# Moving the mixer's squares to another buffer, and bias, sines, filter banks and a normalization to other steps of the attention loop

## The chip, the core and the metric

The kernel runs on one core of one Trainium2 chip. The metric is the device time of one execution in microseconds. The kernel before takes 1604.8 us (median of three runs, 1603.25 to 1608.38). Everything is float32.

The core has engines that run side by side, each in its own order: TensorE (PE in the profile, with its weight loads as PEld), VectorE (DVE), ScalarE (ACT), GpSimd (POOL), and SyncE (SP), which here only issues DMAs. Engines wait for each other through semaphores.

## The reference, cut to what matters

Two layers on x of 8 sequences (b) of 1024 tokens with 128 channels.

```python
# layer 0: attention over the tokens of each sequence
x = x + conv_attn(group_norm(x))        # q, k l2-normalized over tokens; softmax(10 q k); w_out; + b_out
# layer 1, on tokens t
t = t + mamba(layer_norm(t)) + reversed(mamba'(reversed(layer_norm(t))))   # state-space mixer
t = t + spectral(layer_norm(t))         # 16 long filters as FFTs, banks M_phi mixed by 4 weights
```

Of the mixer, per sequence and direction: project to z, x, B, C and dt; a convolution of four taps and silu; a scan in chunks of 64 tokens with decays `exp(segsum(dt*A))`; add `D*x`; multiply by `silu(z)`; normalize by the mean of the squares; project out.

## The kernel before, in words

The program is one stream of instructions per engine. In the attention and the mixer the order is written out by hand: a `manual_schedule` keeps PE, DVE, ACT and POOL in the order in which the Python code emits them. Python generators (`qkv`, `mixer_and_bank`, `transforms`, `transform_taps`, `weighted`) hold side work that is advanced with `next(...)` at chosen steps, so the place of a `next` decides what an instruction stands behind on its engine.

**Attention.** `units` has 128 steps n: 8 sequences, two halves of 512 queries, 8 blocks of 128 keys. A step computes scores (`scores`, L618 on PE into PSUM `pt`, exponential L623 on ACT into `pr`), adds weighted values for the step before (`weigh`, L639), and at every second step sums pairs of `pr` on DVE (`two`, L648) for the denominators (L659). Beside this, by n modulo 16:

- `qkv(b)` prepares a later sequence: transposes (L536), copy (L538), statistics (L543), group norm's rsqrt on POOL (`gn`, L128 and L130) at step 3, scaling of `xnt` (L561, DVE) at 5, q at 6, the squares of q (L580, ACT) at 7, k at 10, the squares of k at 11 and then POOL's lengths (`inv`, L583 and L585), scaling of k (L600, DVE) at 13. The bias `bout` is added to X on POOL (L539), directly after the copy at step 14.
- `mixer_and_bank` (`mixing`): prepares mixer weights and mixes the filter banks M_u and M_phi of the spectral part with weights from a softmax (`select_bank`, a chain of tiny DVE instructions, L214 to L240). The mixing itself is POOL work: `mixed` (L251 and L253) and `both` (L272). It has 32 pieces; seven are advanced per 16 steps.
- `transforms` (`making`) computes angle tables: integers by POOL, casts (L306), range reduction on DVE, sines on ACT (L300). `inv` and `fwd` get their sines before the loop, the four `lags` tables at n = 73.
- At n = 99 and 115 statistics for the mixer's first two sequences, at 103 and 119 the normalization itself (`normalized`, L454): eight activations on ACT in a row.

**Mixer.** 16 units (b, d), two directions for each sequence. A unit's order on PE around the change: transposes of x (`sx`), of B with the product of B and C (`sb`), for d = 0 with a sequence to follow also the transposes of its tokens (`px`); the decays between tokens of a chunk (`pl`, L932); for d = 0 the dt projection of the next sequence (`pd`, L488); decays from a chunk's start (`pe`, L950), chunk states (`pst`, L970), and later the outputs (`sy`, L1039). `between` turns `pl` into `lm` with an exponential on ACT (L939). `pl`, `pd` and `pe` take turns in two PSUM buffers (`ps_w`), so the first matmul after `pl` needs the first `lm` exponential to have read its buffer. ACT loads a table of functions before that exponential. `gate` writes the squares `u.sq` (L1063, ACT) from y; `square_sums` sums them on PE (`misc`, L1081) at the unit's end. All these tiles are from pools in which a tag names one buffer: `sq` has the tag `lm`, so squares and decays share a buffer.

Of the kernel before, what the change touches and what calls it, by code (L numbers as in the profile page):

```python
# [8 lines left out]
F32 = mybir.dt.float32  # L9
AF = mybir.ActivationFunctionType  # L10
ALU = mybir.AluOpType
# [3 lines left out]
P = 128  # L15
B = 8
T = 1024
NT = T // P
C = 128
# [25 lines left out]
def fast_kernel(ctx: ExitStack, tc: tile.TileContext, a: dict, out: bass.AP, bad: bass.AP):  # L45
# [252 lines left out]
    def sines(dst):  # L298
        dst = dst.rearrange("p k i m -> p (k i m)")
        nc.scalar.activation(dst, dst, AF.Sin, scale=-2048.0 * PI_1024)  # L300
# [8 lines left out]
    def transforms(pool, tables):  # L309

        odd = counted(pool, [2, NF], [[512, 2], [2, NF]], 1, 0, "odd")
        place = counted(pool, [4], [[1, 4]], 0, 4, "place")
        odd_row = counted(pool, [1], [[1, 1]], 1, 2, "odd_row")
        places = counted(pool, [4, P], [[1, 4], [4, P]], 0, 0, "places")
        lag = counted(pool, [2, 2], [[-256, 2], [1, 2]], 510, -2, "lag")
        for t in (place, odd_row, lag):
            nc.vector.tensor_scalar(t, t, 1.0 / 2048.0, None, ALU.mult)
        yield
        yield from angles(pool, inv, [(inv, places, odd_row[:, 0:1])], "inv")
        yield  # L320
        yield from angles(
            pool, fwd, [(fwd[:, k : k + 1], odd[:, 0:1, :], place[:, k : k + 1]) for k in range(4)], "fwd"
        )
        yield
        for h in range(2):
            for r in range(2):
                t = pool.tile([P, 2, 2, NF], F32, name=f"lags{h}_{r}")
                for _ in angles(pool, t, [(t, odd, lag[:, h, r : r + 1])], f"lags{h}_{r}"):
                    pass
                tables.append(t)  # L330
                yield
        for t in tables:
            sines(t)

    def transform_taps(pool, ps, tables):
# [113 lines left out]
    def normalized(b, pool, mv, rstd):  # L449
        shift = pool.tile([P, NT], F32, tag="ln_s", name=f"b_shift{b}")  # L450
        nc.vector.scalar_tensor_tensor(shift, mv[:, :, 0], -1.0, rstd, ALU.mult, ALU.mult)
        xn = pool.tile([P, NT, C], F32, tag="ln_x", name=f"b_x{b}")
        for j in range(NT):
            nc.scalar.activation(  # L454
                xn[:, j, :], X[b][:, j, :], AF.Identity, bias=shift[:, j : j + 1], scale=rstd[:, j : j + 1]
            )
        return xn

    n2 = 2 * NH
    pad = KC - 1  # L460
# [57 lines left out]
    with ExitStack() as s:  # L518
# [12 lines left out]
        def qkv(b):  # L531

            xin = X[b]
            pt = ps_t.tile([P, T], F32, tag="t", name=f"xt{b}")
            for j in range(NT):
                nc.tensor.transpose(pt[:, j * P : (j + 1) * P], xin[:, j, :], ident)  # L536
            xt = p1.tile([P, T], F32, tag="xnt", name=f"xnt{b}")
            nc.vector.tensor_copy(xt, pt)  # L538
            nc.gpsimd.tensor_tensor(xin, xin, bout.unsqueeze(1).to_broadcast([P, NT, C]), ALU.add)  # L539
            yield  # L540
            st = p2.tile([P, 2, 6], F32, tag="st", name=f"st{b}")
            for i in range(2):
                nc.vector.bn_stats(st[:, i, :], xt[:, i * 512 : (i + 1) * 512])  # L543
            mv = p2.tile([P, 2], F32, tag="mv", name=f"mv{b}")
            nc.vector.bn_aggr(mv, st.rearrange("p i s -> p (i s)"))
            yield
            pm = ps_t.tile([P, 1], F32, tag="t", name=f"pm{b}")
            nc.tensor.matmul(pm, lhsT=group, rhs=mv[:, 0:1], start=True, stop=True)
            mean = p2.tile([P, 1], F32, tag="mean", name=f"mean{b}")
            nc.vector.tensor_copy(mean, pm)  # L550
            dm = p2.tile([P, 1], F32, tag="dm", name=f"dm{b}")
            nc.vector.tensor_tensor(dm, mv[:, 0:1], mean, ALU.subtract)
            nc.vector.scalar_tensor_tensor(dm, dm, dm, mv[:, 1:2], ALU.mult, ALU.add)
            yield
            pv = ps_t.tile([P, 1], F32, tag="t", name=f"pv{b}")
            nc.tensor.matmul(pv, lhsT=group, rhs=dm, start=True, stop=True)
            var = p2.tile([P, 1], F32, tag="var", name=f"var{b}")
            nc.vector.tensor_copy(var, pv)
            rstd = rsqrt(p2, var, 1, 1.0, 1e-5, "gn")
            yield  # L560
            nc.vector.tensor_scalar(xt, xt, mean, rstd, ALU.subtract, ALU.mult)  # L561
            yield

            ss = p2.tile([P, 2], F32, tag="ss", name=f"ss{b}")
            for i, (name, dst) in enumerate((("q", qs), ("k", ks))):
                pq = ps_t.tile([P, T], F32, tag="t", name=f"p{name}{b}")
                for n in range(2):
                    nc.tensor.matmul(
                        pq[:, n * 512 : (n + 1) * 512],
                        lhsT=wqkv[:, i * C : (i + 1) * C],  # L570
                        rhs=xt[:, n * 512 : (n + 1) * 512],
                        start=True,
                        stop=True,
                    )
                to = keepq.tile([P, T], F32, tag=name, name=f"{name}{b}")
                nc.vector.tensor_copy(to, pq)
                dst.append(to)
                yield
                junk = p1.tile([P, T], F32, tag="junk", name=f"junk{name}{b}")
                nc.scalar.activation(junk, to, AF.Square, accum_out=ss[:, i : i + 1])  # L580
                if i == 0:
                    yield
            nc.gpsimd.tensor_scalar(ss, ss, 1e-24, None, ALU.max)  # L583
            lengths = p2.tile([P, 2], F32, tag="inv", name=f"inv{b}")
            nc.gpsimd.tensor_tensor(lengths, ss, mhalf.to_broadcast([P, 2]), ALU.pow)  # L585
            yield
            pvl = ps_t.tile([P, NT, P], F32, tag="t", name=f"pvl{b}")
            for j in range(NT):
                nc.tensor.matmul(
                    pvl[:, j, :],  # L590
                    lhsT=xt[:, j * P : (j + 1) * P],
                    rhs=wqkv[:, 2 * C : 3 * C],
                    start=True,
                    stop=True,
                )
            v = keepq.tile([P, NT, P], F32, tag="v", name=f"v{b}")
            nc.scalar.copy(v.rearrange("p j d -> p (j d)"), pvl.rearrange("p j d -> p (j d)"))
            vs.append(v)
            yield
            nc.vector.tensor_scalar(to, to, lengths[:, 0:1], lengths[:, 1:2], ALU.mult, ALU.mult)  # L600
# [90 lines left out]
        for at in range(10):  # L691
            next(coming)
            if at in (1, 2, 3, 4, 5, 7):
                next(making)
        for t in (inv, fwd):
            sines(t)
        next(coming, None)
        coming = qkv(1)
        next(coming)
# [1 line left out]
        for n in range(len(units) + 2):  # L701
# [16 lines left out]
                coming = qkv(n // 16 + 2)  # L718
            if n % 16 in (14, 15, 1, 3, 5, 6, 7, 10, 11, 12, 13):
                next(coming, None)  # L720
            if n % 16 in (0, 2, 4, 6, 8, 10, 14):
                next(mixing, None)
            if n >= 16 * (B - 1):
                next(going, None)
# [3 lines left out]
            if n in (99, 115):  # L728
                norm = normalize(bridge, n // 112)
            elif n in (103, 119):  # L730
                xns[n // 112] = normalized(n // 112, bridge, *norm)
            elif n == 113:
                turn_tokens(0, seqs[0], ps_t.tile([P, T], F32, tag="t", name="px0"))
            elif n == 117:
                sizes = steps(0, seqs[0], ps_t.tile([P, T], F32, tag="t", name="pd0"))
                next(sizes)
            elif n in (121, 123):
                next(sizes, None)
# [10 lines left out]
    with ExitStack() as s:  # L749
# [297 lines left out]
        def gate(u, n):  # L1047

            if n == 0:
                u.y = p1.tile([P, 2, T], F32, tag="y", name=f"y{u.tag}")  # L1050
                u.sq = p1.tile([P, 2, T], F32, tag="lm", name=f"sq{u.tag}")
            by_chunk = "p (j c l) -> p c j l"
            for c in range(2):
                nc.vector.scalar_tensor_tensor(
                    u.y[:, n, :].rearrange(by_chunk, j=NT, c=2)[:, c],
                    u.xs[:, n, :].rearrange(by_chunk, j=NT, c=2)[:, c],
                    dcol[u.d][:, n : n + 1],
                    u.py[c][:, n],
                    ALU.mult,
                    ALU.add,  # L1060
                )
            nc.vector.tensor_tensor(u.y[:, n, :], u.y[:, n, :], u.zs[:, n, :], ALU.mult)
            nc.scalar.activation(u.sq[:, n, :], u.y[:, n, :], AF.Square)  # L1063
# [69 lines left out]
        for at, u in enumerate(units):  # L1133
# [14 lines left out]
                going = steps(fresh, seqs[fresh], wide_psum(ps_w, f"pd{fresh}"))  # L1148
                next(going)
            if u.d == 1 and u.b + 2 < B:  # L1150
                xns[u.b + 2] = normalized(u.b + 2, bridge, *norms.pop(u.b + 2))
            from_start(u, 0)
            chunk_states(u)
            pass_states(u)
# [1122 lines left out]
```

## Time and profile before

| stretch (us from the start) | what | PE busy | DVE busy | ACT busy | POOL busy | granted clock |
|---|---|---|---|---|---|---|
| 0 to 32.7 | start, up to the first exponential | 13.18 | 22.60 | 9.06 | 15.92 | 0.93 |
| 32.7 to 472.5 | attention | 422.51 | 340.53 | 285.92 | 217.33 | 0.98 |
| 472.5 to 1153.7 | mixer | 634.43 | 518.18 | 374.62 | 109.00 | 0.97 |
| 1153.7 to 1606 | spectral part | 392.61 | 275.08 | 197.04 | 98.55 | 0.94 |

The rows come from the view of busy times by stretch; the span of the profiled execution is 1605.8 us. Read it from PE: in attention and mixer it is busy over nine tenths of the time, so what matters is the few microseconds at which PE stands still or runs at a lower clock, and who kept it. A granted clock of 1.00 is full speed.

### The profile page before, as it was taken

To read this page: it belongs to the slowest core of one execution; us is meant where nothing else is said; L and a number is where in the kernel's file an instruction comes from. 1 tells how busy PE (TensorE), PEld (TensorE's weight loads), DVE (VectorE), ACT (ScalarE), POOL (GpSimd) and SP (SyncE) were. 2 spreads that over 40 slices of the span, in tenths; PEclk is the share of its full clock that TensorE was granted. 3 is DMA by queue.
4 is the path that set the end of the run, shared out by engine and by line. 5 is a ranking of instruction groups with operands and counts; after the bars stand their busy time and mean duration, and the time that the engine had idled before them with its cause. 6 is when DMAs were issued, how large, how long until landed. Compare 5 with 4: busy or idle time off the path is not lost. (4 is left out here: it accounts for less than half of the span.)

```text
span 1605.8 us, 45749 instructions
## 1 busy us (share of the span) xinstructions
PE 1462.7 (91%) x20118; PEld 886.4 (55%) x20118; DVE 1156.4 (72%) x2314; ACT 866.6 (54%) x1229; POOL 440.8 (27%) x488
## 2 busy tenths in 40 slices
PE   5999999999997999999999999999477899999977
PEld 2323332332334565566565565555367899989862
DVE  6688988777665778787878778778453477777754
ACT  3756665766565456565565656555153265555530
POOL 3299899111110102121212121111064411111100
PEclk8999999999999899999999999999778999999988
DMA  6111121000000010101010010101157623223248
GB/s 164 34 31 50 53 67 40 1 1 1 1 1 13 2 27 14 27 14 28 14 25 16 14 27 14 27 14 27 42 174 208 194 53 82 73 63 86 70 117 309
DMA packets 131960, 89.05 MB, mean 55 GB/s; under 512 B 41480, under 2 KB 114824, under 8 KB 131752
## 3 DMA queue, kind: packets, MB, share of 16 engines
q1 hardware_dynamic: 129640, 81.84, 18.7%
q8 instruction: 160, 2.62, 0.7%
q10 hardware_dynamic: 2112, 4.19, 0.7%
q14 instruction: 48, 0.39, 0.1%
HBM read 44.60 MB, written 33.55 MB: 49 GB/s over the span
## 5 line engine op out<-in xcount | busy, mean ns | idle before, releaser
L623 ACT ACTIVATE pr<-pt 128x1024 f32<-128x1024 f32 x256 | 248.2, 1021 | 131.6 <-PE pt L618 124.5
L648 DVE TENSOR_TENSOR two<-pr,pr 128x1024 f32<-128x1024 f32 x128 | 163.4, 1317 | 14.9 <-ACT pr L623 13.6
L1349 DVE COPY gs<-pg 128x512 f32<-128x512 f32 x256 | 159.7, 686 | 20.0 <-PE pg L1338 13.0
L1351 ACT COPY gs<-pg 128x512 f32<-128x512 f32 x256 | 134.1, 599 | 71.6 <-PE pg L1338 53.1
L618 PE MATMUL pt<-q,k 32*128 32x512 f32 x1024 | 159.9, 656 | 11.0 <-ACT pr L623 6.6
L1338 PE MATMUL pg<-taps,mst 32*128 32x128 f32 x4096 | 150.7, 284 | 9.1 <-ACT gs L1351 4.9
L1338 PEld LDWEIGHTS pg<-taps,mst 32*128 32x128 f32 x4096 | 136.6, 190 | 23.4 <-issue 17.6
L639 PE MATMUL po<-pr,v 128*32 128x512 f32 x1024 | 144.2, 610 | 0.0
L824 DVE SCALAR_TENSOR_TENSOR xs<-xp,cw,xs 128x1024 f32<-128x1024 f32 x96 | 123.1, 1283 | 7.5 <-ACT xs L816 5.2
L1372 PE MATMUL py<-gs,u 128*32 128x128 f32 (+1 forms) x4096 | 127.9, 277 | 0.2 <-DVE gs L1349 0.2
L1372 PEld LDWEIGHTS py<-gs,u 128*32 128x32 f32 (+1 forms) x4096 | 112.1, 140 | 7.5 <-DVE gs L1349 0.4
L844 PE MATMUL pb<-bxt,wbc 128*128 128x512 f32 x256 | 114.2, 598 | 0.3 <-ACT zs L835 0.3
L1099 POOL TENSOR_TENSOR rms<-rms_v,mhalf 128x8 f32<-128x8 f32 x16 | 39.2, 2453 | 269.1 <-DVE rms_v L1097 269.1
L778 POOL TENSOR_TENSOR dau<-upto,da 128x2048 f32<-128x2048 f32 x16 | 57.9, 3620 | 158.9 <-DVE state L984 158.9
L618 PEld LDWEIGHTS pt<-q,k 32*128 32x128 f32 x1024 | 47.3, 187 | 89.9 <-issue 34.4
L1361 POOL TENSOR_SCALAR u<-u 128x512 f32<-128x512 f32 x16 | 24.0, 1498 | 233.7 <-PE pg L1338 119.9
L987 DVE SCALAR_TENSOR_TENSOR state<-state,dec,pst 128x64 f32<-128x64 f32 x448 | 87.3, 275 | 1.1
L659 PE MATMUL pd<-two,ones 128*32 128x512 f32 x512 | 78.8, 619 | 4.4 <-DVE two L648 4.0
L844 PEld LDWEIGHTS pb<-bxt,wbc 128*128 128x128 f32 x256 | 47.1, 189 | 56.0 <-issue 53.8
L639 PEld LDWEIGHTS po<-pr,v 128*32 128x32 f32 x1024 | 28.8, 110 | 89.1 <-issue 85.1
L950 PE MATMUL pe<-dau,ones 64*64 64x512 f32 x256 | 69.7, 668 | 8.8 <-ACT lm L939 6.6
L1039 PEld LDWEIGHTS sy<-lm,xdt 64*64 64x64 f32 x2048 | 59.9, 139 | 29.8 <-DVE ec L1013 15.2
(279 smaller groups left out, 2863.9 us busy)
## 6 DMA issues: line engine op xcount, KB each, us to landing
ud<-sp SPq DMA_DIRECT2D x8, 1024.0 KB
u<-ud SPq DMA_DIRECT2D x32, 256.0 KB
yd<-sums SPq DMA_DIRECT2D x32, 256.0 KB
moved<-state SPq DMA_DIRECT2D x48, 128.0 KB
yt<-yd SPq DMA_DIRECT2D x6, 1024.0 KB
X<-in_x SPq DMA_DIRECT2D x8, 512.0 KB
part_p<-in_L_ffn_M_phi_plus SPq DMA_DIRECT2D x32, 128.0 KB
part_m<-in_L_ffn_M_phi_minus SPq DMA_DIRECT2D x32, 128.0 KB
```

The lines of the kernel that those rows point to most:

```text
L618: nc.tensor.matmul(pt[:, i, :], lhsT=k[rows, j * P : (j + 1) * P], rhs=q[rows, cols], start=True, stop=True)
L623: nc.scalar.activation(pr[:, 2 * g : 2 * g + 2, :].rearrange("p i t -> p (i t)"), pt.rearrange("p i t -> p (i t)"), AF.Exp, scale=SCALE,)
L639: nc.tensor.matmul(po[rows, :], lhsT=vs[b][:, j, rows], rhs=pr[:, h, :], start=(j == 0), stop=(j == NT - 1))
L648: nc.vector.tensor_tensor(two, sums["pr"][:, 2 * g : 2 * g + 2, :], pr[:, 2 * g : 2 * g + 2, :], ALU.add)
L659: nc.tensor.matmul(sums["d"][(2 * g + i) * DH : (2 * g + i + 1) * DH, :], lhsT=ones[:, :DH], rhs=two[:, i, :], start=(j == 1), stop=(j == ...
L824: nc.vector.scalar_tensor_tensor(acc, xp[:, at : at + T], cw[u.d][:, n, i : i + 1], acc, ALU.mult, ALU.add)
L844: nc.tensor.matmul(u.pb[:, i * 512 : (i + 1) * 512], lhsT=wbc[u.d][:, k, :], rhs=xt[:, at : at + 512], start=(k == 0), stop=(k == KC - 1),)
L987: nc.vector.scalar_tensor_tensor(u.state[:, k, h, :], u.state[:, k - 1, h, :], u.dec[:, c, j, h : h + 1], u.pst[c][:, j, h, :], ALU.mult, ...
L1338: nc.tensor.matmul(pts[g][:, e, :], lhsT=mst[rows, n * 4 + e, :], rhs=taps[rows, cols].rearrange("p f q m i -> p (f q m i)"), start=True, ...
L1349: nc.vector.tensor_copy(to, frm)
L1351: nc.scalar.copy(to, frm)
L1372: nc.tensor.matmul(py[t * 32 : t * 32 + 32 - 16 * m, q // 2, :], lhsT=u[:, i, m:, :, :, q * FC + f].rearrange("p k b i -> p (k b i)"), rhs ...
```

## The change

The change has two parts. The squares of the mixer take the buffer of the decayed x (`xdd`), not that of the decays (`lm`). In the attention loop the bias addition goes from the copy at step 14 to after the squares of q at step 7; the sines of `inv` are emitted before the first squares of q and those of `fwd` together with the `lags` tables at n = 73; one cast and three scalings of the tables go behind the first sequence's copy and statistics; the mixing of the banks is advanced five times per 16 steps, at 4, 6, 8, 12 and 14 (so it ends at n = 102 instead of n = 72, and the DVE chain of `select_bank` goes from n = 14 to n = 22); and the mixer's normalization is split into halves, at n = 103 and 105, and at 119 and 122. No arithmetic is added or removed. The aim is that instructions that stand behind others on their engine, without needing them, no longer do.

```diff
@@ transforms
         places = counted(pool, [4, P], [[1, 4], [4, P]], 0, 0, "places")
+        yield
         lag = counted(pool, [2, 2], [[-256, 2], [1, 2]], 510, -2, "lag")
         for t in (place, odd_row, lag):
             nc.vector.tensor_scalar(t, t, 1.0 / 2048.0, None, ALU.mult)
-        yield
...
-        for t in tables:
+        for t in (fwd, *tables):
             sines(t)
@@ normalized
         for j in range(NT):
+            if j == NT // 2:
+                yield
             nc.scalar.activation(
@@ qkv
             nc.vector.tensor_copy(xt, pt)
-            nc.gpsimd.tensor_tensor(xin, xin, bout.unsqueeze(1).to_broadcast([P, NT, C]), ALU.add)
...
                 nc.scalar.activation(junk, to, AF.Square, accum_out=ss[:, i : i + 1])
                 if i == 0:
+                    nc.gpsimd.tensor_tensor(xin, xin, bout.unsqueeze(1).to_broadcast([P, NT, C]), ALU.add)
                     yield
@@ before the loop
-        for t in (inv, fwd):
-            sines(t)
+            if at == 4:
+                sines(inv)
@@ the loop
-            if n % 16 in (0, 2, 4, 6, 8, 10, 14):
+            if n % 16 in (4, 6, 8, 12, 14):
                 next(mixing, None)
...
-                xns[n // 112] = normalized(n // 112, bridge, *norm)
+                norming = normalized(n // 112, bridge, *norm)
+                next(norming)
+            elif n in (105, 122):
+                next(norming, None)
@@ gate
-                u.sq = p1.tile([P, 2, T], F32, tag="lm", name=f"sq{u.tag}")
+                u.sq = p1.tile([P, 2, T], F32, tag="xdd", name=f"sq{u.tag}")
```

More of the change, by code (lines that the diff above doesn't have):

```diff
@@ L451, in normalized @@
         nc.vector.scalar_tensor_tensor(shift, mv[:, :, 0], -1.0, rstd, ALU.mult, ALU.mult)
-        xn = pool.tile([P, NT, C], F32, tag="ln_x", name=f"b_x{b}")
+        xn = xns[b] = pool.tile([P, NT, C], F32, tag="ln_x", name=f"b_x{b}")
         for j in range(NT):
+            if j == NT // 2:
+                yield
             nc.scalar.activation(
@@ L456, in normalized @@
             )
-        return xn
     n2 = 2 * NH
@@ L1150, in fast_kernel @@
             if u.d == 1 and u.b + 2 < B:
-                xns[u.b + 2] = normalized(u.b + 2, bridge, *norms.pop(u.b + 2))
+                for _ in normalized(u.b + 2, bridge, *norms.pop(u.b + 2)):
+                    pass
             from_start(u, 0)
```

## The prediction

> **What bounds the kernel now.** I read the page first: PE is busy 91% of the span. The busy times by stretch then show that attention and mixer are PE's, and that POOL's load differs between sequences. Two sequences of the attention loop side by side, b = 3 and b = 5 (columns: stretch, its length, busy time of PE, PEld, DVE, ACT, POOL, granted clock, DMA):
>
> ```profile
> 194.70:251.00 56.30, 52.33 (x377) 17.50 (x380) 46.01 (x53) 34.12 (x37) 53.45 (x51) 1.00 0.20 57
> 306.20:356.20 50.00, 50.00 (x376) 16.63 (x379) 39.31 (x49) 34.01 (x37) 6.60 (x5) 1.00 0.00 1
> ```
>
> The same PE and ACT work takes 50.0 us where POOL is empty and 56.3 where it is full. Measured from exponential to exponential, the eight sequences (b = 0 to 7) take 51.7, 56.2, 54.1, 56.3, 55.2, 50.0, 55.0 and about 60 us; 50.0 is the floor. The timeline says who held PE:
>
> ```profile
> 160.86 0.94 DVE L561 TENSOR_SCALAR xnt<-xnt,mean,gn 128x1024 f32<-128x1024 f32 x1 [4.26 <-POOL gn L130]
> ...
> 161.95 1.95 PE L568 MATMUL pq<-xnt,wqkv 128*128 128x512 f32 x4 [2.27 <-DVE xnt L561]
> ...
> 381.44 3.18 ACT L454 ACTIVATE b_x<-X,b_shift,ln_r 128x128 f32<-128x128 f32 x8
> ```
>
> DVE sat 4.26 us for POOL's rsqrt, which stood behind mixing, and PE 2.27 us for DVE. Later ACT spends 3.18 us on the normalization at a stretch.
>
> ```profile
> 7.55 2.34 POOL L539 TENSOR_TENSOR X<-X,bout 128x1024 f32<-128x1024 f32 x1
> 7.59 2.32 DVE L306 CAST lag<-lag_i 128x4 f32<-128x4 int32 x1 [0.23 <-POOL lag_i L304]
> ...
> 27.54 2.35 POOL L539 TENSOR_TENSOR X<-X,bout 128x1024 f32<-128x1024 f32 x1
> 27.61 2.83 DVE L600 TENSOR_SCALAR k<-k,inv 128x1024 f32<-128x1024 f32 x1 [0.91 <-POOL inv L585]
> ```
>
> A cast of four columns lasts 2.32 us and the scaling of k 2.83 (its fastest is 0.71): both started just after a bias addition on POOL and ended with or just after it.
>
> In the mixer I asked for the decays' line and for one unit on ACT and PE:
>
> ```profile
> L939 ACT ACT_TABLE_LOAD  x16: 1283/1283/1283, 501.0 to 1122.5; - x16
> L939 ACTq EVENT_SEMAPHORE  x15: 17/17/17, 553.1 to 1122.4; - x15
> ```
>
> ```profile
> 715.53 0.58 ACT L910 COPY bk<-sb 128x512 f32<-128x512 f32 x1 [4.03 <-PE sb L902]
> 717.48 1.28 ACT L939 ACT_TABLE_LOAD   x1 [1.36 <-PE pl L932]
> 718.77 1.94 ACT L939 ACTIVATE lm<-pl 128x1024 f32<-128x1024 f32 x2
> ```
>
> ```profile
> 715.41 3.70 PE L932 MATMUL pl<-dau,row_lt 128*128 128x512 f32 x8
> 719.85 0.65 PE L950 MATMUL pe<-dau,ones 64*64 64x512 f32 x2 [0.73 <-ACT lm L939]
> ```
>
> The table load, which needs no data, waits 1.36 us for `pl`; the exponential comes after it, and PE idles 0.73 us for the buffer. This repeats in 15 of 16 units, those with an event semaphore at L939.
>
> ```profile
> 758.82:761.99 3.17, 2.12 (x18) 1.87 (x17) 0.25 (x2) 1.76 (x2) 0.00 (x0) 1.00 0.55 165
> 761.99:767.20 5.21, 5.21 (x73) 2.92 (x75) 0.59 (x3) 1.28 (x2) 0.00 (x0) 0.67 0.01 3
> 719.85:723.36 3.51, 3.51 (x72) 2.41 (x74) 0.27 (x2) 3.51 (x9) 0.00 (x0) 1.00 0.00 0
> ```
>
> In a d = 0 unit the idle gap is followed by `pd`, sixteen matmul records of eight columns; then `pe` and `pst` take 5.21 us at a mean clock of 0.67, against 3.51 at 1.00 in the d = 1 unit.
>
> [...]
>
> **The change part by part.**
>
> 1. *Squares in `xdd`'s buffer.* In the built order before, `lm`'s exponential has two waits, ACT's own earlier `sq` (same buffer) and PE's `pl`, and the one for `pl` is placed ahead of the table load. In the changed order `lm` has the wait for `pl` alone, directly at the exponential, and the table load has none. It can start when `bk` is copied, 716.11, and end by 717.39, before `pl`'s first half at 717.48. The exponential starts 717.48 instead of 718.77, its first half (1.02) ends at 718.50. `pl`'s last matmul starts at 718.52 and the next can follow about 0.43 later (their spacing), 718.95 instead of 719.85: 0.90 us. In d = 0 units the copy before is `bxt`, ended 755.88; load until 757.18, `pl` ready 757.35, so the same 0.90. Sum 15 x 0.90 = 13.5; the idle time alone is 15 x 0.73 = 11. The new sharing makes the next `xdd` wait for `misc`'s matmuls, but its own input `xdt` needs the transposes `sx` behind them on PE, so nothing is added; behind `xdd` on DVE stand `gm` and the residual, which then wait for nothing new. What follows on DVE (28 state steps of 0.2 to 0.3 us) starts from `pst`, thus moves with PE. I take 12.
>
> 2. *The clock in d = 0 units.* The nearly empty stretch goes from 3.17 to 2.27 us. [...] Six such units lose 5.21 - 3.51 = 1.7 us each, 10 in all. I take 7, range 0 to 10.
>
> 3. *Start.* Without cast and scalings ahead, the copy of the first `xnt` starts near 7.4 instead of 10.03; with 0.4 given back behind the statistics, group norm is 2.0 to 2.3 earlier. But the bias addition now stands right behind `gn` on POOL and meets L561: 0.81 becomes about 2.8, and 2.0 is lost[...]. L600 at 27.61 then meets an idle POOL, 0.8 instead of 2.83, and the first scores start 2.0 earlier. The exponential's table must be loaded by then: `inv`'s sine (1.06) lies in ACT's 21.1 us of idle time, `fwd`'s is gone from here, one table load less. I take -2.0 (0 to -4).
>
> 4. *Bias and mixing.* With pieces at 4, 6, 8, 12, 14 none is queued ahead of `gn` at 3 or the lengths at 11, and POOL gets 5/7 of the load. The 21.8 us above the floor in b = 1 to 4 hold 3.8 for the lags' sines, about 5 for the `select_bank` chain around n = 14 to 17, and about 13 for waits on POOL's queue and held `two`s. I expect 9 of the 13 back. b = 5 and most of b = 6 now have POOL work: +0.7 each, +1.4. The chain at n = 22 still delays av behind it but no longer stands behind a bias addition (L214 took 1.28): -2.
>
> 5. *Sines.* `fwd` at n = 73 stands between exponentials: 1.04 on ACT, +1.0.
>
> 6. *Normalization in halves.* The lump held PE 2.02 us at 385.57 and 2.60 at 448.42, and the clock was at half from there. A half is 1.6 us, of which the step's spare ACT time (2.9 less 2.0) takes about 0.9. I take -2.5 and -3.0.
>
> Sum: -12 - 7 - 2 - 9 + 1.4 - 2 + 1 - 5.5 = -35.1. 1604.8 - 35 = 1570. The spectral part isn't touched.
>
> **The rivals.**
> - *Clock not healed, half of the POOL gain*: -11 for the mixer's gaps, -11 for attention: 1583. For it: [...]most bank work still meets DVE.
> - *Everything at its upper value*: -13.5 - 10 - 22 = 1559. For it: every PE gap named is one with PE as head of the chain.
> - *Mixer bound elsewhere*: PE's gap reappears at a wait for DVE or ACT (`pp` waits for `ec` 0.34 us per unit already), so only attention gains, 12: 1593. Against: DVE idles 3.49 us before the state copy.
> - *Slower*: bias additions meet `two` or L561 in every sequence (8 x 2.0 = +16), b = 5 and 6 rise by 3 each, `fwd` +1, and the mixer gains 11: about +12, or 1617 with no clock healed and the spectral part's start unchanged. Against: `two` has slack in most steps, and PE's waits on DVE in b = 1 to 4 were 7.9 us in all.
>
> **How the numbers follow.** Forecast 0.55, first rival 0.20, upper values 0.12, mixer elsewhere 0.09, slower 0.04. The range 1556 to 1590 holds the first three and most of the fourth's edge. Faster 0.94, same 0.02, slower 0.04.
>
> **What would show it.** In the changed trace: L939's table loads wait for nothing and `pe` and `pd` no longer wait for `lm`; `pe` and `pst` of d = 0 units at clock 1.00; L561's first instance about 2.8 us, L600's about 0.8; no DVE wait for `gn` or `inv` over 1 us; b = 1 to 4 at 51 to 55 us. The forecast is wrong if a unit of the mixer keeps its length, or if b = 5 and 6 grow past 53 and 56.

## The result and the profile after

The changed kernel takes 1567.22 us (median of four runs, 1565.97 to 1567.81), against 1604.97 for the kernel before: a ratio of 0.9761, 95% interval 0.9744 to 0.9779. In the two profiled executions the span goes from 1605.8 to 1566.0 us. From the page of the changed kernel, its span, the busy time of its engines and the granted clock in 40 slices:

```profile
span 1566.0 us, 45729 instructions
...
PE 1446.0 (92%) x20118; PEld 884.1 (56%) x20118; DVE 1153.0 (74%) x2314; ACT 867.2 (55%) x1228; POOL 443.9 (28%) x488
...
PEclk8999999999998999999999999999698999999988
```

PE lost 16.7 us of busy time (1462.7 before) with the same 20118 matmuls, and by the clock records of the two traces the clock stood at half for 126.8 us before and 95.7 after. So part of the gain is clock and the rest is idle time. Marking the same four instructions in both traces shows where the 39.8 us of span went:

| stretch | before | after | difference |
|---|---|---|---|
| start to first exponential of the attention | 32.7 | 30.4 | -2.3 |
| first to last exponential of the attention | 435.9 | 420.7 | -15.2 |
| to the first `lm` exponential of the mixer | 33.7 | 34.8 | +1.1 |
| first to last `lm` of the mixer | 621.4 | 596.7 | -24.7 |
| to the end | 482.1 | 483.4 | +1.3 |

The +1.1 goes with a half clock of 3.4 us at 477.0 that the kernel before has not. In the traces of all kernels below, this stretch takes 34.8 to 35.6 us where it holds such a half clock and 33.7 or 33.8 where it holds none.

**Mixer.** The line of the decays in the changed kernel (durations are lowest, median and highest in ns, then the first and the last start in us):

```profile
L943 ACT ACT_TABLE_LOAD  x16: 1283/1283/1283, 484.6 to 1081.3; - x16
```

The 15 event semaphores of L939 before are gone. One d = 1 unit, on ACT and then on PE (start, duration, in brackets idle time and what ended it):

```profile
690.96 0.58 ACT L914 COPY bk<-sb 128x512 f32<-128x512 f32 x1 [4.03 <-PE sb L906]
691.57 1.28 ACT L943 ACT_TABLE_LOAD   x1
692.87 1.02 ACT L943 ACTIVATE lm<-pl 128x1024 f32<-128x1024 f32 x1
```

```profile
690.85 3.70 PE L936 MATMUL pl<-dau,row_lt 128*128 128x512 f32 x8
694.48 1.50 PE L954 MATMUL pe<-dau,ones 64*64 64x512 f32 x5
```

The table load follows the copy of `bk` with no wait, and is over when `pl` is half done. `pe` comes 3.63 us after `pl` began; it was 4.44 in the unit of before that the prediction shows. The stretches of a d = 0 unit that answer to those of the prediction (the nearly empty one with `pd`, then `pe` and `pst`), and last `pe` and `pst` of a d = 1 unit, all from the changed kernel (length, busy time of PE, PEld, DVE, ACT, POOL, clock, DMA):

```profile
733.45:735.61 2.16, 1.85 (x17) 1.75 (x15) 0.24 (x2) 1.02 (x1) 0.00 (x0) 1.00 0.78 223
735.61:739.13 3.52, 3.52 (x73) 2.42 (x74) 0.60 (x3) 1.28 (x2) 0.00 (x0) 1.00 0.07 17
694.48:697.99 3.51, 3.51 (x73) 2.54 (x74) 1.07 (x5) 3.37 (x8) 0.00 (x0) 1.00 0.00 0
```

The empty stretch fell from 3.17 to 2.16 us, and the 5.21 us at 0.67 became 3.52 at 1.00. From `lm` to `lm`, most intervals that end in a d = 0 unit went from 39.87 to 39.07, and most of those that end in a d = 1 unit, and hold the half clock of the d = 0 unit before it, from 42.29 to 39.60.

**Attention.** Exponential to exponential, the sequences b = 0 to 7 take (the last one to its last exponential):

| b | 0 | 1 | 2 | 3 | 4 | 5 | 6 | 7 |
|---|---|---|---|---|---|---|---|---|
| before | 51.7 | 56.2 | 54.1 | 56.3 | 55.2 | 50.0 | 55.0 | 57.4 |
| after | 51.2 | 54.7 | 51.1 | 51.0 | 55.6 | 50.5 | 52.1 | 54.4 |

The busy times of b = 3 and b = 5 in the changed kernel:

```profile
187.34:238.37 51.03, 51.03 (x376) 16.78 (x379) 44.83 (x54) 34.17 (x37) 36.43 (x34) 1.00 0.15 44
293.99:344.53 50.54, 50.54 (x376) 17.03 (x380) 41.27 (x50) 34.05 (x37) 39.67 (x38) 1.00 0.15 44
```

POOL's 53.45 us of b = 3 became 36.43, its 6.60 of b = 5 became 39.67, and both sequences lie within 1.1 us of the 50.0 that an empty POOL gave. Who waited, from 32 to 345 us, in the view of waits (total us, times, longest): first DVE for POOL in the kernel before, then in the changed one.

```profile
DVE xnt L561 <- POOL gn L130: 8.9, 4, 4.3
DVE k L600 <- POOL inv L585: 7.8, 3, 4.4
```

```profile
DVE xnt L561 <- POOL gn L130: 0.4, 1, 0.4
```

PE's own waits in the same stretch, again before and then after, fell from 12.2 us in all to 5.4; those for `two` and `xnt` are gone (the two largest of before, and all of after):

```profile
PE pd L659 <- DVE two L648: 4.0, 4, 2.3
PE pq L568 <- DVE xnt L561: 3.9, 2, 2.3
```

```profile
PE pt L619 <- ACT pr L624: 3.0, 1, 3.0
PE py L425 <- DVE av L680: 2.4, 1, 2.4
```

POOL has as much work as before (443.9 us busy in all, 440.8 before), but hardly anything that DVE needs stands behind it.

### The profile page after: what moved, and what is told of

Its sections match the earlier page's. It is cut to its first block, busy times and chain, and to the rows that moved or that the text cites. A ratio compares the mean times of both kernels' runs of the same rounds, so it can differ in the third digit from the quotient of the medians.

```text
span 1566.0 us, 45729 instructions
## 1 busy us (share of the span) xinstructions
PE 1446.0 (92%) x20118; PEld 884.1 (56%) x20118; DVE 1153.0 (74%) x2314; ACT 867.2 (55%) x1228; POOL 443.9 (28%) x488
## 4 chain that ended last, share of the span: by engine, by line
PE 84%; DVE 5%; ACT 4%; DMA 3%; issue 2%; POOL 2%; SPq 0%; DVEq 0%; ACTq 0%; POOLq 0%
PE pg L1343 9%; PE pt L619 9%; PE py L1377 8%; PE pb L848 7%; PE po L640 7%; PE sy L1043 4%; PE pd L660 4%; PE spo L1073 4%; PE pl L936 4%; PE pz L799 4%; PE pp L799 4%; PE pe L954 3%; PE sb L906 2%; PE pu L1307 2%; PE pst L974 2%
## 5 line engine op out<-in xcount | busy, mean ns | idle before, releaser
L1043 PEld LDWEIGHTS sy<-lm,xdt 64*64 64x64 f32 x2048 | 59.6, 138 | 29.5 <-DVE ec L1017 15.2
L660 PE MATMUL pd<-two,ones 128*32 128x512 f32 x512 | 74.7, 612 | 0.2
L1043 PE MATMUL sy<-lm,xdt 64*64 64x64 f32 x2048 | 66.3, 227 | 5.5 <-DVE lm L1013 5.5
```

Source lines behind the costliest of these rows:

```text
L660: nc.tensor.matmul(sums["d"][(2 * g + i) * DH : (2 * g + i + 1) * DH, :], lhsT=ones[:, :DH], rhs=two[:, i, :], start=(j == 1), stop=(j == ...
L1043: nc.tensor.matmul(u.py[c][h * HP : (h + 1) * HP, r, j, :], lhsT=left, rhs=right, start=(kind == 0), stop=(kind == 1 or k is None),)
```

## The experiments

All compute the whole result. Where a ratio is given, the kernel ran several times; any other time is that of one execution. Beside the three groups of runs the kernel before took 1611.09 us (median of seven), 1608.35 (one run) and 1612.22 (median of nine, 1605.33 to 1613.94), so a single time is worth less than the stretches of its trace.

**The two parts alone.**

```diff
 # squares_only: the kernel before, with
-                u.sq = p1.tile([P, 2, T], F32, tag="lm", name=f"sq{u.tag}")
+                u.sq = p1.tile([P, 2, T], F32, tag="xdd", name=f"sq{u.tag}")
 # attention_only: the changed kernel, with the opposite edit
```

> The kernel before, with the squares in the buffer of the decayed x and nothing else changed. Theory (the wait for pl no longer stands ahead of the table load, so pe or pd follow pl at once, and the stretch ahead of pe in d = 0 units becomes too short to halve the clock): the mixer's 621 us from first to last lm shrink by about 24.7 us, as in the changed kernel (d = 0 units 42.3 to 39.6 us, d = 1 units 39.9 to 39.1), and the ratio is about 0.985. Rival (the mixer's gain needed the attention part[...]): d = 0 units stay near 42.3 minus 0.8, the mixer gains 12 us, ratio 0.992.

> The changed kernel with the squares back in the buffer of the decays. Theory: the two parts are independent. The attention loop's last exponential starts at about 451 us, as in the changed kernel, instead of 468.6; the mixer takes about 621 us from first to last lm; ratio about 0.990 (16 us). Rival (they help each other): the mixer is shorter than 615 us.

Squares alone: 1589.12 us, ratio 0.986 (0.9831 to 0.9888), mixer 597.8 us, the sequences of the attention as before but for b = 0 (50.6, with a half clock of 10.2 us instead of 13.7 at the start) and b = 2 (55.8). Attention part alone: 1592.48, ratio 0.9888 (0.9862 to 0.9915), last exponential at 451.1 us as in the changed kernel, mixer 622.0 with half clock back in six d = 0 units. 0.986 x 0.9888 is 0.975, and each part leaves the stretches of the other alone: the parts don't touch each other.

**Is it the buffer, or the table load?** The squares stay in the buffer of the decays, so `lm` keeps both waits, but a one-column exponential of a constant, which nothing reads, calls for the table earlier:

```diff
 # early_load: the kernel before, ahead of the decays
+            early = p1.tile([P, 1], F32, tag="early", name=f"early{u.tag}")
+            nc.scalar.activation(early, ones[:, 0:1], AF.Exp)
```

> The kernel before, squares still in the buffer of the decays, with one exponential of 128x1 ahead of the decays' exponential, which makes the table load come there and wait for nothing; it writes a tile of its own that nothing reads. Theory (what cost the time is the table load standing behind the wait for pl): the mixer shrinks by about 24 us from first to last lm, all but the 16 tiny activations (0.2 to 0.3 us each, beside PE), ratio about 0.985. Rival (the shared buffer itself costs, through the write after the squares' read): the mixer stays at 621 us, ratio 1.00.

1587.5 us, ratio 0.9858 (0.9834 to 0.9882); mixer 597.9 us, intervals 39.03 and 39.65. ACT in one unit:

```profile
710.48 1.28 ACT L928 ACT_TABLE_LOAD   x1
711.77 0.20 ACT L928 ACTIVATE early<-ones 128x1 f32<-128x1 f32 x1
711.88 1.01 ACT L941 ACTIVATE lm<-pl 128x1024 f32<-128x1024 f32 x1
```

The view of L941 still counts 15 event semaphores, and the whole gain is there. So the sharing of the buffer itself costs nothing that can be seen; what cost was that the load stood behind the wait for `pl`.

**Gap and half clock apart.** Two kernels give only the units of one direction the new buffer:

```diff
 # freed_d1: the kernel before, with
+                u.sq = p1.tile([P, 2, T], F32, tag="lm" if u.d else "xdd", name=f"sq{u.tag}")
 # freed_d0: the kernel before, with
+                u.sq = p1.tile([P, 2, T], F32, tag="xdd" if u.d else "lm", name=f"sq{u.tag}")
```

The squares of one unit delay the decays of the next, so the first one frees the d = 1 units.

> The kernel before, with the squares of d = 0 units in the buffer of the decayed x and those of d = 1 units left in that of the decays: only the exponential of d = 1 units is freed of its second wait. Theory: d = 1 units lose 0.8 us each, d = 0 units keep their gap ahead of pd, and most of them keep the half clock after it (they stay within 0.3 us of 42.3); the mixer gains 5 to 8 us. Rival[...]: the d = 0 units drop to about 40.4 although their gap is still there.

> The kernel before, with the squares of d = 1 units in xdd's buffer, so that the decays of the following d = 0 units have no wait on an own earlier instruction. If the gap and the half clock are one chain, then the intervals that end in d = 0 units lose 0.8 us, the half clocks of the d = 0 units go (1.9 us each), and the intervals that end in d = 1 units keep their gap: about 7 x 0.8 + 6 x 1.9 = 17 us less in the mixer (621 to about 604). Rival: the half clock comes from the eight-column matmuls of the dt projection whatever the gap; then the half clocks stay and the mixer loses 6 us.

With d = 0 freed, the mixer takes 604.3 us (expected about 604). A pair of units takes 79.48 us, 2.69 less than the 82.17 before: 0.90 for the gap ahead of `pd`, 0.11 from the start of `pd` to that of `pe`, and 1.69 for the half clock, of which none is left after the first unit. The line of the decays has eight event semaphores, one for each d = 1 unit:

```profile
L939 ACT ACT_TABLE_LOAD  x16: 1283/1283/1283, 504.2 to 1108.5; - x16
L939 ACTq EVENT_SEMAPHORE  x8: 17/17/17, 555.7 to 1108.5; - x8
```

With d = 1 freed (1602.87 us), the mixer takes 611.4 us: 10.0 less, where 5 to 8 were expected. Four of the six half clocks stayed and two went, though the empty stretch is as long as before in all of them. The intervals with a half clock take 40.96 us and those without 39.27, so a half clock alone costs 1.69. Two d = 0 units, each as the empty stretch and then `pe` and `pst`:

```profile
758.58:761.75 3.17, 2.12 (x17) 1.86 (x17) 0.24 (x2) 1.76 (x2) 0.00 (x0) 1.00 0.55 165
761.75:766.95 5.20, 5.20 (x73) 3.50 (x75) 0.59 (x3) 1.28 (x2) 0.00 (x0) 0.67 0.01 3
839.94:843.11 3.17, 2.12 (x18) 1.86 (x17) 0.25 (x2) 1.76 (x2) 0.00 (x0) 1.00 0.55 165
843.11:846.62 3.51, 3.51 (x72) 2.41 (x74) 0.59 (x3) 1.28 (x2) 0.00 (x0) 1.00 0.02 5
```

The same work, the same 3.17 us, once 5.20 us after it and once 3.51. The clock records of the traces show where the two differ. In the trace of the kernel before, the half clocks of the six d = 0 units start at 598.40, 680.32, 762.24, 844.16, 926.08 and 1008.00 us, each 81.92 after the last, which is 24 times 3.413; here they start at 680.81, 762.73, 923.15 and 1005.07, which is 24, 47 and 24 times 3.413. Each of these lasts 3.41 us. I counted on from them in steps of 3.413 us. Of the first of the two stretches, 2.44 us, or 0.71 of a step, lie in the one step that ends at 762.73, where half clock sets in. The second is divided at 841.23, 23 steps later, into 1.29 and 1.88 us, or 0.55 of a step at most. Each trace has seven such stretches with `pd`, and the 14 traces together 98. The 16 with 0.69 of a step or more inside one step were all followed by half clock, and the 82 with 0.64 or less were not. This is a count over these traces; what lowers the clock they don't show. The 2.16 us of the changed kernel are 0.63 of a step, and in all six units the clock stayed at 1.00.

**How often the bank mixing is advanced.**

```diff
 # mixing_dense: the changed kernel, with
-            if n % 16 in (4, 6, 8, 12, 14):
+            if n % 16 in (0, 2, 4, 6, 8, 10, 14):
```

> The changed kernel with the mixing of the banks advanced at seven steps of 16 again (0, 2, 4, 6, 8, 10, 14). Theory (most of the gain in b = 1 to 4 comes from POOL's queue being empty at group norm's rsqrt and at the lengths): DVE again waits 3 to 4 us for gn in b = 2 and 3, sequences b = 2 and 3 rise from 51 to 53 or more, b = 5 falls to 50.0, and the last exponential starts 5 to 9 us later than 451.1. Rival (the bias's place did it): b = 2 and 3 stay within 0.7 of 51.

1581.34 us; the last exponential comes 9.2 us later, just above what was expected, and b = 1 to 4 take 58.4, 52.6, 53.3 and 57.3 us (in b = 4 with a half clock of 6.8 us instead of 3.4). The edit also takes the chain of `select_bank` back to n = 14, so the 9.2 us hold that too. The waits for `gn` that I expected did not come (1.7 us in three). The wait is at the lengths of k instead: DVE, and POOL in the same microseconds.

```profile
133.17 0.95 DVE L601 TENSOR_SCALAR k<-k,inv 128x1024 f32<-128x1024 f32 x1 [4.42 <-POOL inv L586]
```

```profile
131.30 0.72 POOL L253 TENSOR_TENSOR minus<-minus,part_m 128x256 f32<-128x256 f32 x1
132.11 0.22 POOL L584 TENSOR_SCALAR ss<-ss 128x2 f32<-128x2 f32 x1
132.41 0.72 POOL L586 TENSOR_TENSOR inv<-ss,mhalf 128x2 f32<-128x2 f32 x1
```

The piece of step 10 stands ahead of the lengths of step 11. In all, `k` waits 5.7 us for the lengths in this kernel from 32 to 345 us, and PE 4.4 us in eight waits for `two`; the changed kernel has none of either there.

**Where the bias is added.**

```diff
 # bias_at_copy: the changed kernel, with
             nc.vector.tensor_copy(xt, pt)
+            nc.gpsimd.tensor_tensor(xin, xin, bout.unsqueeze(1).to_broadcast([P, NT, C]), ALU.add)
 # and not after the squares of q; bias0_at_copy: so for the first sequence alone
```

> The changed kernel with the bias addition back behind the copy of xnt, the mixing left at five of 16. Theory (the bias's place matters less than the mixing's): b = 1 to 4 stay within 1 us of the changed kernel's, 54.7, 51.1, 51.0 and 55.6. At the start the first L561 falls from 2.83 to about 0.8 us and L601 rises to 2.8, so the first exponential stays at 30.4 plus or minus 0.5. Rival (the bias addition holding a sum of pairs cost the 3 us at the end of b = 3 before): one of b = 1 to 3 rises by 2 us or more.

> The changed kernel, with the bias addition of the first sequence alone back at its copy. If the first sequence's L561 and k scaling are each held only when a bias addition starts just before them, then both take about 0.8 us here (L561 2.83 before in the changed kernel), the first exponential comes at 28.2 to 29.2 us instead of 30.4, the sequences after the first keep their lengths of the changed kernel within 0.7 us, and the last exponential is 1 to 2 us earlier. Rival: the bias addition runs into the transposes' copy of the second sequence or the scaling again, and the first exponential stays at 30 to 31 us.

All at the copy: 1573.15 us, first exponential at 29.08 (1.3 earlier; I had expected no change), last at 452.7 (1.6 later), with b = 2 and b = 4 longer by 1.8 and 2.1 (in b = 4 the half clock lasts 6.8 us instead of 3.4) and b = 0 shorter by 1.2 (half clock 6.8 instead of 10.2). Neither expectation fits whole. The first sequence alone: first exponential at 28.35 and both scalings at 0.81 us, as expected; the sequences keep their lengths but b = 4 (57.2, half clock for 6.8 us instead of 3.4) and b = 7 (55.0), and the last exponential is at 450.9, only 0.2 us earlier. The 2.0 us of the start were given back in these two, where the half clocks of the shifted program lay otherwise (b = 7 has one at 433.3 that the changed kernel has not).

**Where `fwd` gets its sines.**

```diff
 # fwd_early: the changed kernel, with
-        for t in (fwd, *tables):
+        for t in tables:
 # and, behind the first sequence's preparation
+        sines(fwd)
```

> The changed kernel with the sines of fwd emitted right after the first sequence's preparation, ahead of the exponentials' table, not at n = 73. Theory (fwd's sine lengthens ACT's stretch at n = 73[...] and the half clock at 275.6 follows; at the start it is free): the first exponential stays at 30.4 within 0.3, b = 4 falls from 55.6 to 51.9 to 53.5 and no half clock is granted near 275. Rival (the lags' sines alone do it): b = 4 falls by 1.0 or less and the half clock stays.

1570.54 us. The first exponential stays at 30.4, b = 4 takes 54.7 instead of 55.6, and its half clock stays (at 274.9), so the sine of `fwd` is not what causes that. The last exponential is 1.3 us earlier; the time is longer only because the untouched part behind the mixer took 487.3 us here, not 483.4.

**The normalization in one piece.**

```diff
 # norm_whole: the changed kernel, with both halves at 103 and 119
                 next(norming)
-            elif n in (105, 122):
                 next(norming, None)
```

> The changed kernel with each of the first two normalizations in one piece again, at n = 103 and 119. Theory (the lump of 3.2 us on ACT starves PE and brings the half clock): b = 6 rises from 52.1 to about 55.0 and b = 7 from 54.4 to about 57.4, with half clock granted near 375 and 433; the last exponential starts near 457. Rival (the halves only divide the same loss): both rise by less than 1.5.

1580.85 us; b = 6 and 7 take 55.3 and 57.7 (+3.2, +3.3), with half clocks at 377.4 and 438.9. b = 4, which the edit leaves alone, took 1.6 us more too, with a half clock of 6.8 us instead of 3.4. PE's wait for the exponentials from 360 us on, first in this kernel, then in the changed one:

```profile
PE pt L619 <- ACT pr L624: 4.6, 2, 2.6
```

```profile
PE pt L619 <- ACT pr L624: 1.6, 2, 1.1
```

**A further version.** `best` joins bias0_at_copy and fwd_early; `after_again` is the changed kernel beside it.

> Both start edits together: the first bias addition at its copy, and the sines of fwd before the loop. Expected from bias_at_copy (first exponential 1.3 us earlier) and fwd_early (last exponential 1.3 us earlier): last exponential near 448.5 us, 2 to 3 us less than the changed kernel in all, ratio to the kernel before 0.973 to 0.977. Rival: the start's gain is given back in later sequences by another meeting of POOL and DVE, and the kernel is within 0.5 us of the changed one.

> The changed kernel itself, for comparison on the same chip: last exponential at 451 us, ratio to the kernel before 0.974 to 0.978.

`best` takes 1563.82 us (1563.16 to 1566.32, five runs; ratio 0.9709, 0.9688 to 0.9731), the changed kernel 1567.11 (1563.74 to 1568.80, five; 0.9722, 0.970 to 0.9745). Both ratios lie below what was expected, because the kernel before was slower beside these runs; the changed kernel's own median is that of the first runs. The median of `best` is 3.3 us lower, but the ranges overlap, so a small gain is likely and not proven. In the trace the last exponential is at 446.9 us, 4.2 us before that of the changed kernel. The first scalings of `xnt` and k take 0.81 us each, which makes 2.0 us. Another 3.6 come in b = 0 (47.6 us), where the half clock of the start lasts 3.4 us instead of 10.2, and b = 1, 4 and 7 give 1.6 back. The 3.6 can't be counted on: in the two traces of the changed kernel itself that half clock lasts 10.2 and 13.7 us.

## Why the prediction was right, step by step

The forecast was 1570, the time 1567.2. The likeliest case is the one that came; by stretches it gave -16 for the attention with its start (measured -17.5) and -19 for the mixer (-24.7). The traces moved by more than the medians: the two stretches that were put at no change took 2.4 us more, and the profiled execution of the kernel before was the slowest of its four (1608.38 us). That the sum came so near is in part luck.

1. *Squares, -12: right.* early_load shows the mechanism, the waits of L943 are gone, and from the start of `pl` to the next matmul a unit without `pd` gains 0.81 us and one with `pd` 0.90; nine of the first and six of the second make 12.7. I had worked out 0.90 for all, with 0.43 from `pl`'s last matmul to the next one; in the units without `pd` it is 0.52 (693.96 to 694.48).
2. *Clock, -7, range 0 to 10: right in kind, at the upper end of the range.* All six units were healed. The price of 1.7 us for each was right: four gained 1.69 and two, whose half clock began just before `pe`, 1.56 and 1.50, which makes 9.8. What was too small was the 7, my own discount for the doubt whether all six would be spared, with no measurement behind it. After 3.17 us, freed_d1 kept the half clock in four of six; after 2.16 us the changed kernel has it in none of six. The rest of the mixer's 24.7 us is 0.11 in each of the six between `pd` and `pe`, whose cause is not shown, 0.5 by which the last exponential alone comes earlier, and 1.1 in the first unit. That last part goes with a half clock of 6.8 us there instead of 10.2, and so is not counted as a gain of the edit: in squares_only, where it lasts 10.2, the unit takes the 50.8 us of before.
3. *Start, -2.0: right, with its two halves.* The first copy of `xnt` started at 7.27 instead of 10.03 us, and L561 at 14.82 instead of 17.32; no run tests the moved cast and scalings alone. L561 took 2.83 us beside the bias addition (14.75 to 17.09) right behind `gn`, as worked out, and k's scaling, with no bias addition beside it, 0.81:

```profile
14.82 2.83 DVE L561 TENSOR_SCALAR xnt<-xnt,mean,gn 128x1024 f32<-128x1024 f32 x1 [0.47 <-POOL gn L130]
...
28.08 0.81 DVE L601 TENSOR_SCALAR k<-k,inv 128x1024 f32<-128x1024 f32 x1 [0.92 <-POOL inv L586]
```

The first exponential came 2.3 us earlier. best and bias0_at_copy, in which both scalings take 0.81 us, show that the 2.0 lost here can be had back at the start.
4. *Bias and mixing, -9, +1.4, -2: right in sum, not separated in all parts.* b = 1 to 4 together lost 9.4 us; without `fwd`'s share of step 5 that is 10.3, for the -11 of these terms. mixing_dense gives 9.2 back, so the places of the pieces, with that of the chain, carry most of it; the place of the bias is worth 2.9 after the first exponential (bias_at_copy: 1.6 + 1.3), with the differences of half clock named there. b = 5 grew by 0.5, and b = 6, whose normalization is worth 3.2, fell by 2.9: +0.8 where I took +1.4. For the -2 of the `select_bank` chain no run stands alone. In the two traces the steps n = 16 and 17, behind the chain's old place, went from 11.5 to 6.4 us, but n = 22, 24 and 25, at the new one, from 10.1 to 13.9: most of the cost moved with the chain, and 1.3 us net were saved. PE still waits for `av` behind it once, 2.4 us.

5. *Sines, +1.0: right* (fwd_early: 0.9). The changed kernel around n = 73, ACT and then what PE waited for:

```profile
268.77 1.06 ACT L300 ACTIVATE fwd<-fwd 128x1024 f32<-128x1024 f32 x1
269.74 2.17 ACT L300 ACTIVATE lags<-lags 128x512 f32<-128x512 f32 x4
```

```profile
274.30 2.63 PE L619 MATMUL pt<-q,k 32*128 32x512 f32 x8 [2.98 <-ACT pr L624]
```

The wait is followed by a half clock at 275.6, which the kernel before did not have there. b = 4 ended at 55.6, above the 51 to 55 I had named as the mark; without `fwd`'s sine (fwd_early) it takes 54.7, still with the half clock, so 0.9 of what it takes more than b = 2 and 3 is the sine of `fwd`, and the rest goes with the sines of `lags` and the half clock, which no run tells apart.
6. *Normalization, -2.5 and -3.0: right* (norm_whole: 3.2 and 3.3). A half takes 1.64 us of ACT between two exponentials (1.6 was taken).

The spectral part, which I had put at no change, took 1.3 us more in the profiled run, and 482 to 491 us in the traces of all these kernels, though its instructions are the same. The length of its half clocks doesn't tell these apart (72.0 us before, 71.7 after, 67.8 where it took 490.6), and the difference doesn't come at one place: where it took 490.6, the lag behind the kernel before grows from 2.1 us, 100 us into this part, to 7.9 us at 340. The cause stays open. The two traces of the changed kernel have 483.4 both. It is one reason why single times here carry some 7 us that no edit made.

The rivals: clock not healed fell with the six half clocks, the mixer bound elsewhere with the whole 0.81 or 0.90 in every unit, and slower with b = 5 and b = 6, which stayed below 53 and 56. Everything at its upper value came close in the mixer (12.7 of 13.5 and 9.8 of 10) and not in the attention (17.5 of 22).

## What to carry to other kernels

When an engine must switch its table of functions before an instruction that waits for data, look at whether the load itself sits behind that wait: an early, empty call of the function, or one wait fewer on the instruction, lets it run beside the producer, as here the load of 1.28 us beside `pl` (mixer 621.4 us before, 597.9 in early_load, 597.8 in squares_only). Work on GpSimd was cheap here by its amount and dear by its place (POOL's 440.8 us became 443.9, while VectorE's waits for `gn` and `inv` from 32 to 345 us fell from 16.7 to 0.4): list the short results that VectorE needs from it, and put no long piece ahead of them. And when removing an idle gap of PE, count the clock behind it, which here was worth more than three quarters of the gaps (9.8 against 12.7 us).

## What the runs showed of the hardware

- A table load of 1.28 us stood behind the wait for `pl` where the exponential had two waits, and ahead of it where it had one (15 event semaphores at L939 before, none at L943 after, eight in freed_d0).
- The half clock after an empty stretch of 3.17 us came in four of six equal cases and not in two (freed_d1); after 2.16 us in none of six. In the clock records the half clocks of one trace start whole multiples of 3.413 us apart (24 times in the kernel before; 24, 47 and 24 times in freed_d1). Counted in steps of 3.413 us from them, the 16 of the 98 stretches with `pd` that had 0.69 of a step or more inside one step were followed by one, the 82 with 0.64 or less were not. Behind such a stretch a half clock costs 1.69 us (40.96 against 39.27, freed_d1).
- A scaling of `xnt` or k took 2.83 us with a bias addition on POOL beside it and 0.81 without (the first `xnt` in the changed kernel and in bias0_at_copy, the first k in the kernel before and in the changed one); why, the traces don't show.
- In a program shifted by 2 us, a half clock in b = 4 lasted 6.8 us instead of 3.4 (bias0_at_copy).
- The half clock at the start lasts 3.4, 6.8, 10.2 or 13.7 us in the traces of these kernels, and the first sequence takes 47.6, 50.0, 50.6 to 51.2 and 51.7 to 52.0 us with it (best; bias_at_copy; the changed kernel and others; the kernel before, after_again and freed_d1).
